# A graph network on one core: normed node values made before the adjacency, three strips, the preparations of the messages moved into the second convolution, and pools that wait by tile

## The chip, the cores and the metric

The program runs on one core of one Trainium2 chip. The metric is the device time of one execution in microseconds (us), as the median of several runs. Each profile is of one execution, with its own time beside its span. PE is TensorE (PEld its weight loads), DVE VectorE, ACT ScalarE, POOL GpSimd, SP SyncE; SPq, ACTq and POOLq are DMA issues of these engines.

## What is computed

There are N = 6250 nodes with 64 features and E = 206250 edges, sorted by their target `dst`. Every edge stands in both directions, and each node has one to itself. Ahead of each of four layers the node values are normed. Cut to what matters:

```python
h = maximum(layernorm(x), 0); x = x + conv(conv(h, W3, b3, relu), W4, b4)   # D^-1/2 (A+I) D^-1/2
h = maximum(layernorm(x), 0); x = x + segment_sum(norm * h[col], row)
h = maximum(layernorm(x), 0)
Vp = leaky_relu(leaky_relu(h) @ pAw + pAb) @ pBw + pBb
e = relu(relu(E @ w1 + b1) @ w2 + b2)
msg = sigmoid(e @ Bw + Bb) * Vp[src] + (e @ Cw + Cb)
x = x + sqrt(segment_mean(clip(msg, 1e-5) ** 2, dst))
h = maximum(layernorm(x), 0); acc = h
for _ in range(3): h = segment_sum(norm * h[row], col); acc = acc + h
x = x + acc / 4
```

## The kernel before

The nodes are padded to 49 blocks of 128, in 7 chunks of 7 blocks (`blocks(c)`, 896 nodes). The kernel builds the matrix A of edge counts, 6272 x 6272, as fp8, and every sum over edges but that of the messages is a product with it. Node values that are multiplied with A are split into three bf16 parts (`split`, L709: two copies on ACT, two subtractions on DVE for a chunk), kept in U3 or V3.

**Stage 1: edges to keys, degrees (L751 to L921).** The edge ends are combined to one number per edge, written to DRAM, and read back by 25 rough and 25 exact searches: `near` (a broadcast of samples), 25 comparisons on DVE (L802), then for each column group an indirect gather by POOL (L864), a comparison (L868), a second gather (L873), digits, transposes, and `key`. The loop at L871 also builds the first strip. When all 25 groups are done, the degrees follow (L904 to L919), and from them `norm0` and `norm3`.

**Stage 2: A in 14 strips of 448 columns, and the first convolution (L923 to L990).** First, for each chunk, `normed` (L691: three passes and two small steps on DVE, a square root on ACT, a last pass) of X, times `norm0`, and `split` into U3. `build(s, q)` makes 32 columns of strip s: two comparisons on DVE (L844, `hd` and `lo`), 16 matmuls into `p_a` (L853), two copies to fp8 on ACT (L857). 14 of these make a strip, and `convolve(s)` multiplies it with U3 (147 matmuls, L748), while strip s+1 is built. The strip goes to DRAM (L984). Every two strips `hidden(c)` turns the sums of one chunk into V3 by small matmuls and transposes (L737 to L967). `spool` has 2 strips.

**Stages 3 and 4: two gathers (`gather`, L998).** For each of 7 chunks, 7 pieces of A (128 x 7 x 896, loaded by SP, 8 buffers) are multiplied with V3 or U3: 343 matmuls (L1013) into four banks `p_acc`, opened by products with zeros (L1010) and summed up by DVE (L1021). Then `convolved` (L1035) finishes the chunk of the second convolution, norms it and splits it into a new U3; `turned` (L1053) in stage 4 adds the second layer, norms, and computes Vp by PE (L1062, L1067, L1073), ACT (L1065, L1069) and DVE (L1070, L1076, L1078), and SP writes it to DRAM (L1079).

**Preparations of the messages (L1085 to L1157).** Weights and biases are put into place (biases as three bf16 parts, L1113 to L1120). `src` and `dst` are loaded with `p` as the partition: each partition takes 8 edges of every one of 202 groups (L1125, L1127), runs of 32 bytes. From dst come a check that each group's targets lie in a window of 128 nodes (POOL's 194 memsets of `origin`, L1133, and L1136 to L1142 on DVE) and the `lane` of each edge (L1145, L1147).

**Stage 5: messages (L1158 to L1414).** 202 groups of 1024 edges go through a software pipeline, `slot(i)` (L1350): POOL fetches the rows of Vp by 8 indirect gathers (L1276, 4 buffers of `v`), PE, ACT and DVE take the edge features through the small network, gate them with v, square, and sum to the nodes. Beside this, PE and DVE compare A with its transpose, and PE does parts of the next layer's sums. On PE, ACT and DVE the order of this stage is written out by hand (`manual_schedule`, L1396). Everywhere else, and on POOL and SP throughout, a planner orders the instructions: it may run an instruction ahead of others on its engine when its inputs and its memory are free, and prefers those that come first in the program. Each engine then runs its list in order.

**Stage 6: the three propagations (L1417 to L1462)**, the first from sums already made, the others by `gather`.

Pools are opened and closed as a stack in SBUF and PSUM, so a new pool takes the memory of closed ones. By default, an instruction that first uses the new pool's memory waits for the pools that lay there before.

Of the kernel before, what the change touches and what calls it, by code (L numbers as in the profile page):

```python
# [8 lines left out]
F32 = mybir.dt.float32  # L9
BF16 = mybir.dt.bfloat16  # L10
# [6 lines left out]
P = 128  # L17
N = 6250
D = 64
# [597 lines left out]
def fast(ctx, tc, bad, x, src, dst, edge_attr, W3, b3, W4, b4, w1, b1, w2, b2, Bw, Bb, Cw, Cb,  # L617
# [48 lines left out]
    node = ctx.enter_context(tc.tile_pool(name="node", bufs=1))  # L666
    stat = ctx.enter_context(tc.tile_pool(name="stat", bufs=2))
# [3 lines left out]
    def blocks(c):  # L671
        return slice(c * CB, (c + 1) * CB)

    def over_features(v, n=CB):
        return v.unsqueeze(2).to_broadcast([P, n, D])
# [15 lines left out]
    def normed(h, X_c):  # L691

        m = stat.tile([P, CB], F32, name="m")
        nc.vector.tensor_reduce(m, X_c, axis=AX.X, op=OP.add)
        nc.vector.tensor_scalar_mul(m, m, 1.0 / D)
        nc.vector.tensor_sub(h, X_c, over_features(m))
        q = stat.tile([P, CB, D], F32, name="q")
        nc.vector.tensor_mul(q, h, h)
        v = stat.tile([P, CB], F32, name="v")
        nc.vector.tensor_reduce(v, q, axis=AX.X, op=OP.add)  # L700
        nc.scalar.activation(v, v, AF.Sqrt, bias=eps, scale=1.0 / D)
        nc.vector.reciprocal(v, v)
        nc.vector.scalar_tensor_tensor(h, h, 0.0, over_features(v), op0=OP.max, op1=OP.mult)
# [48 lines left out]
    nc.scalar.dma_start(X, x.rearrange("(b p) f -> p b f", p=P))  # L752
    early = ExitStack()
    early_pool = early.enter_context(tc.tile_pool(name="early_pool", bufs=1))
    with ExitStack() as ph:

        ipool = ph.enter_context(tc.tile_pool(name="ipool", bufs=1))
        with ExitStack() as first:
            dpool = first.enter_context(tc.tile_pool(name="dpool", bufs=1))
# [37 lines left out]
        npool = looked.enter_context(tc.tile_pool(name="npool", bufs=1))  # L797
# [11 lines left out]
        rpool = ph.enter_context(tc.tile_pool(name="rpool", bufs=3))  # L809
        opool = ph.enter_context(tc.tile_pool(name="opool", bufs=2))  # L810
        spool = ph.enter_context(tc.tile_pool(name="spool", bufs=2))
        wpool = ph.enter_context(tc.tile_pool(name="wpool", bufs=1))
# [13 lines left out]
        with ExitStack() as ps:  # L826
            psum = ps.enter_context(tc.tile_pool(name="ps0", bufs=1, space=PSUM))
            p = psum.tile([P, 512], F32, name="p_node")
            nc.tensor.transpose(p[:D, :P], W3_sb, ident)
            nc.vector.tensor_copy(W3T, p[:D, :P])  # L830
            p = psum.tile([P, 512], F32, name="p_node")
            nc.tensor.transpose(p[:, :D], W4_sb, ident[:D, :D])
            nc.vector.tensor_copy(W4T, p[:, :D])
# [90 lines left out]
            for c in range(NC):  # L924
                u = wpool.tile([P, CB, D], F32, name="z", bufs=2)
                normed(u, X[:, blocks(c), :])
                nc.vector.tensor_mul(u, u, over_features(norm0[:, blocks(c)]))
                split(u, U3, c)
# [97 lines left out]

    with ExitStack() as ph:
        wpool = ph.enter_context(tc.tile_pool(name="wpool", bufs=2))  # L1030
        U3 = of_nodes(node)
        with tc.tile_pool(name="apool", bufs=8) as apool, \
                tc.tile_pool(name="ps1", bufs=1, space=PSUM) as psum:

            def convolved(c, z):  # L1035
                add_whole(z, V3, c)
                nc.vector.tensor_mul(z, z, over_features(norm0[:, blocks(c)]))
                nc.vector.tensor_add(z, z, over_blocks(b4_r, CB))
                nc.vector.tensor_add(X[:, blocks(c), :], X[:, blocks(c), :], z)
                h = wpool.tile([P, CB, D], F32, name="h")  # L1040
                normed_and_split(h, U3, c, norm3)

            gather(apool, wpool, psum, V3, convolved)
# [6 lines left out]
        with tc.tile_pool(name="apool", bufs=8) as apool, \  # L1050
                tc.tile_pool(name="ps2", bufs=1, space=PSUM) as psum:
# [34 lines left out]
    late = ctx.enter_context(tc.tile_pool(name="late", bufs=1))  # L1086
    H = late.tile([P, NB, D], F32, name="H")
    U3 = of_nodes(node)
    part = ctx.enter_context(tc.tile_pool(name="part", bufs=1))
    Y = part.tile([P, CS, CW], F32, name="Y")  # L1090
    piece_pool = ctx.enter_context(tc.tile_pool(name="piece_pool", bufs=3))
    with ExitStack() as ph:
        cpool = ph.enter_context(tc.tile_pool(name="cpool", bufs=1))
        before = ExitStack()
        tpool = before.enter_context(tc.tile_pool(name="tpool", bufs=1))
        w1_d = diagonal(w1, "w1_d")
        w2_d = diagonal(w2, "w2_d")
        b1_c = column(b1, 2, "b1_c")
        b2_c = column(b2, 2, "b2_c")

        BC = cpool.tile([P, 4 * D], F32, name="BC")
        nc.vector.memset(BC, 0.0)
        for k in range(2):
            nc.scalar.dma_start(BC[k * D:(k + 1) * D, 2 * k * D:(2 * k + 1) * D], Bw)
            nc.scalar.dma_start(BC[k * D:(k + 1) * D, (2 * k + 1) * D:(2 * k + 2) * D], Cw)

        bias = tpool.tile([1, 4, 2, D], F32, name="bias")
        for k in range(4):
            nc.scalar.dma_start(bias[:, k, 0, :], Bb.unsqueeze(0))
            nc.scalar.dma_start(bias[:, k, 1, :], Cb.unsqueeze(0))  # L1110
        rest = tpool.tile([1, 4, 2, D], F32, name="rest")
        bias3 = [tpool.tile([1, 4, 2, D], BF16, name=f"bias{k}") for k in range(3)]
        nc.vector.tensor_copy(bias3[0], bias)  # L1113
        nc.vector.tensor_sub(rest, bias, bias3[0])
        nc.vector.tensor_copy(bias3[1], rest)
        nc.vector.tensor_sub(rest, rest, bias3[1])
        nc.vector.tensor_copy(bias3[2], rest)
        BC_b = cpool.tile([3, 8 * D], BF16, name="BC_b")
        for k in range(3):
            nc.sync.dma_start(BC_b[k:k + 1, :], bias3[k].rearrange("o a b f -> o (a b f)"))  # L1120
        ones = cpool.tile([3, P], BF16, name="ones")
        nc.vector.memset(ones, 1.0)

        src_g = cpool.tile([P, G, J], I32, name="src_g")
        nc.sync.dma_start(src_g, src.rearrange("(g p j) -> p g j", p=P, j=J))  # L1125
        dst_g = tpool.tile([P, G, J], I32, name="dst_g")
        nc.sync.dma_start(dst_g, dst.rearrange("(g p j) -> p g j", p=P, j=J))  # L1127

        origin = tpool.tile([P, G], F32, name="origin")
        g0 = 0  # L1130
        for g in range(1, G + 1):
            if g == G or window(g) != window(g0):
                nc.gpsimd.memset(origin[:, g0:g], float(window(g0) * QN))  # L1133
                g0 = g
        rel = tpool.tile([P, G, J], F32, name="rel")
        nc.vector.tensor_tensor(rel, dst_g, origin.unsqueeze(2).to_broadcast([P, G, J]),  # L1136
                                op=OP.subtract)
        off = tpool.tile([P, G, J], F32, name="off")
        nc.vector.tensor_scalar(off, rel, float(P), None, op0=OP.is_ge)
        nc.vector.tensor_scalar(rel, rel, 0.0, None, op0=OP.is_lt)  # L1140
        nc.vector.tensor_add(off, off, rel)
        nc.vector.tensor_reduce(missed[:, 1:2], off.rearrange("p g j -> p (g j)"), axis=AX.X,  # L1142
                                op=OP.add)

        nc.vector.tensor_scalar(dst_g, dst_g, P - 1, None, op0=OP.bitwise_and)  # L1145
        lane = cpool.tile([P, G, J], BF16, name="lane")
        nc.vector.tensor_copy(lane, dst_g)  # L1147
        own = cpool.tile([P, P // QN, 2], F32, name="own")
        nc.vector.memset(own[:, :, 0], 0.0)
        for q in range(P // QN):  # L1150
            nc.vector.memset(own[q * QN:(q + 1) * QN, :q + 1, 0], 1.0)
        nc.vector.tensor_scalar(own[:, :, 1], own[:, :, 0], -1.0, 1.0, op0=OP.mult, op1=OP.add)
        count = cpool.tile([P, P, J], BF16, name="count")
        nc.gpsimd.iota(count, pattern=[[1, P], [0, J]], base=0, channel_multiplier=0,
                       allow_small_or_imprecise_dtypes=True)

        before.close()  # L1157
        mpool = ph.enter_context(tc.tile_pool(name="mpool", bufs=3))  # L1158
        ps_a = ph.enter_context(tc.tile_pool(name="ps_a", bufs=1, space=PSUM))
# [255 lines left out]


    with ExitStack() as ph:  # L1417
        apool = ph.enter_context(tc.tile_pool(name="apool", bufs=6))
        wpool = ph.enter_context(tc.tile_pool(name="wpool", bufs=2))
        psum = ph.enter_context(tc.tile_pool(name="ps4", bufs=1, space=PSUM))  # L1420
        upool = ph.enter_context(tc.tile_pool(name="upool", bufs=1))
# [82 lines left out]
```

## Time and profile before

| What | us |
|---|---|
| median of 10 runs (lowest to highest) | 3639.87 (3636.82 to 3643.76) |
| profiled execution | 3635.89 |
| its span | 3633.8 |
| busy PE / DVE / ACT / POOL | 3042.0 / 1949.8 / 1243.6 / 1647.0 |
| first and last gather of messages begin | 1074.07, 3148.8 |
| searches begin to be read (L802) | 32.02 |
| first matmul of the first convolution | 151.21 |
| first matmul of `gather`, first time | 596.04 |

In a row of groups one reads line, engine, operation, output and inputs, count, then busy us and mean ns of one, then idle time of the engine just before them, with what ended it. In a timeline row one reads start, duration, engine, line and operation, and in brackets the idle time before it and its releaser. A row that spans a window gives the busy time of each engine in it and the clock that PE was granted as a share of the full one.

### The profile page before, as it was taken

What the parts mean: (1) busy time and instruction counts of PE and PEld (TensorE: products, weight loads), DVE (VectorE), ACT (ScalarE), POOL (GpSimd) and SP (SyncE); (2) the same over time, 40 slices, a digit from 0 to 9 for tenths busy, and PEclk for the clock granted to TensorE, in tenths of its full rate; (3) what the DMA queues carried; (4) which work ended last, traced back from release to release, by engine and by line L of the source; (5) the groups of instructions that cost most, each with busy time, mean ns of one, the idle gap of its engine ahead of it and who ended that gap; (6) DMA issues with size and microseconds to landing.
All of it is one profiled execution on the core that took longest, in us unless ns stands there. A gap on an engine that the chain in (4) does not pass through costs nothing.

```text
span 3633.8 us, 59188 instructions
## 1 busy us (share of the span) xinstructions
PE 3042.0 (84%) x24193; PEld 2135.9 (59%) x24193; DVE 1949.8 (54%) x3904; ACT 1243.6 (34%) x2031; POOL 1647.0 (45%) x1870
## 2 busy tenths in 40 slices
PE   1699999999957777778888788888887878799999
PEld 1466667999944444444444444454444444489999
DVE  5899993332235546555655655655655565531111
ACT  1477772000014334334444433444434344210000
POOL 4100000000027777777777777777777777500000
PEclk9699999999978888888888888888888988899999
DMA  3133335646572222323233223232332323256664
GB/s 112 53 95 94 95 95 174 196 173 197 177 93 73 73 67 67 88 70 94 70 90 85 78 70 88 76 88 70 96 80 78 94 69 79 80 161 196 196 205 143
DMA packets 280495, 388.75 MB, mean 107 GB/s; under 512 B 189225, under 2 KB 191331, under 8 KB 279955
## 3 DMA queue, kind: packets, MB, share of 16 engines
q1 hardware_dynamic: 222260, 323.17, 29.5%
q0 software_dynamic: 54112, 58.92, 8.0%
q8 instruction: 192, 3.15, 0.4%
q10 hardware_dynamic: 3840, 2.77, 0.3%
q14 instruction: 91, 0.75, 0.1%
HBM read 340.47 MB, written 44.24 MB: 106 GB/s over the span
## 4 chain that ended last, share of the span: by engine, by line
POOL 35%; PE 33%; issue 15%; DMA 9%; DVE 6%; ACT 1%; POOLq 0%; DVEq 0%; SPq 0%; ACTq 0%
POOL v L1276 34%; PE p_acc L1013 21%; DMA v<-Vp_dram,src_g 6%; PE p_sum L748 6%; PE p_a L853 3%; DVE hd L844 1%; DVE lo L844 1%; DMA dst_g<-in_dst 1%; PE p_node L739 1%; DMA near<-pairs,begin_i 1%; PE p_bc L1302 0%; PE p_node L957 0%; DMA run<-pairs,exact_i 0%; PE p_acc L1010 0%; PE p_node L962 0%
## 5 line engine op out<-in xcount | busy, mean ns | idle before, releaser
L1276 POOL DMA_INDIRECT v<-Vp_dram,src_g x1616 | 1583.5, 980 | 526.5 <-issue 458.0
L1013 PE MATMUL p_acc<-U,piece 128*128 128x192 bf16 x9604 | 815.7, 247 | 3.0 <-DMA piece<-A 3.0
L1013 PEld LDWEIGHTS <-piece 128*128 128x128 fp8e4 x9604 | 798.2, 98 | 14.7 <-DMA piece<-A 3.8
L1302 PE MATMUL p_bc<-BC,h 128*128 128x256 f32 x1616 | 584.3, 495 | 0.0
L1311 DVE TENSOR_TENSOR m<-gate,v 128x512 f32<-128x512 f32 x202 | 140.0, 693 | 760.2 <-DMA v<-Vp_dram,src_g 330.7
L1302 PEld LDWEIGHTS p_bc<-BC,h 128*128 128x128 f32 x1616 | 341.7, 234 | 156.2 <-issue 117.5
L1133 POOL MEMSET origin<- 128x1 f32 (+1 forms) x194 | 6.5, 97 | 906.9 <-PE p_acc L1013 906.9
L1318 ACT ACTIVATE m<-m 128x512 bf16<-128x512 f32 x202 | 127.2, 630 | 816.3 <-DVE m L1313 816.3
L1021 DVE TENSOR_REDUCE zg<-p_acc 128x128 f32<-128x384 f32 x112 | 56.8, 507 | 598.6 <-PE p_acc L1013 598.0
L748 PEld LDWEIGHTS <-U 128*64 128x64 bf16 x4116 | 233.5, 114 | 236.7 <-issue 93.2
L857 ACT ACTIVATE strip<-p_a 128x784 fp8e4<-128x784 f32 x392 | 301.8, 820 | 105.0 <-PE p_a L853 103.6
L1298 PE MATMUL p_bc<-BC_b,ones 3*128 3x512 bf16 x404 | 182.3, 451 | 169.3 <-DVE m L1312 169.1
L1298 PEld LDWEIGHTS <-ones 3*128 3x128 bf16 x404 | 37.5, 93 | 438.5 <-DVE m L1312 238.2
L1185 PEld LDWEIGHTS <-piece 128*128 128x128 fp8e4 x1372 | 116.0, 106 | 297.2 <-issue 279.5
L1185 PE MATMUL p_sum<-ident_b,piece 128*128 128x128 bf16 x1372 | 152.6, 235 | 163.7 <-DVE junk L1191 163.7
L1288 PE MATMUL p<-h,w_d 128*128 128x512 f32 x404 | 249.0, 701 | 39.4 <-ACT h L1292 39.4
L748 PE MATMUL p_sum<-piece,U 128*64 128x448 fp8e4 x2058 | 239.7, 377 | 39.2 <-DVE junk L1191 29.2
L1292 ACT ACTIVATE h<-p,b_c 128x512 f32<-128x512 f32 x404 | 255.7, 683 | 13.7 <-PE p L1288 13.7
L1191 DVE SCALAR_TENSOR_TENSOR junk<-p_sum,there 128x512 bf16<-128x512 f32 (+1 forms) x392 | 242.1, 618 | 21.4 <-DMA e<-in_edge_attr 8.0
L748 PE MATMUL p_sum<-strip,U 128*64 128x448 fp8e4 x2058 | 243.8, 365 | 8.9 <-ACT U L711 4.6
L844 DVE TENSOR_TENSOR lo<-count,key 128x2048 bf16<-128x2048 bf16 x196 | 238.2, 1215 | 0.0
L853 PEld LDWEIGHTS <-lo 128*128 128x128 bf16 x3136 | 164.9, 103 | 106.8 <-DVE lo L844 86.7
(189 smaller groups left out, 3471.4 us busy)
## 6 DMA issues: line engine op xcount, KB each, us to landing
piece<-A SPq DMA_DIRECT2D x249, 784.0 KB
e<-in_edge_attr SPq DMA_DIRECT2D x202, 256.0 KB
A<-strip SPq DMA_DIRECT2D x14, 2744.0 KB
v<-Vp_dram,src_g POOLq DMA_INDIRECT x1616
there<-A SPq DMA_DIRECT2D x28, 784.0 KB
pairs<-pair SPq DMA_DIRECT2D x1, 1616.0 KB
Vp_dram<-v SPq DMA_DIRECT2D x7, 224.0 KB
out<-X SPq DMA_DIRECT2D x6, 224.0 KB
```

What stands on the lines that cost most here:

```text
L748: nc.tensor.matmul(p[half * D:(half + 1) * D, :w], U3[:, b, k, :], at_block, start=(i < 2), stop=(i >= 3 * n - 2))
L844: nc.vector.tensor_tensor(t, of.unsqueeze(1).to_broadcast(t.shape), key[:, k, at:at + GB].rearrange("p (h j) -> p h j", j=GQ) .unsqueeze(2 ...
L853: nc.tensor.matmul(p[:, j, :2 * NB], lo[:, g // GQ, :, g % GQ], hd[:, g // GQ, :, g % GQ], start=True, stop=True)
L857: nc.scalar.activation(strips[s][:, :, col:col + 2 * SG].rearrange("p b (j l) -> p b j l", l=2), p[:, :, :2 * NB].rearrange("p j (b l) -> ...
L1013: nc.tensor.matmul(p[d // 2][:, d % 2 * 3 * D:(d % 2 + 1) * 3 * D], t[:, b, d * P:(d + 1) * P], U3[:, k * CB + b, :, :].rearrange("p t f - ...
L1185: nc.tensor.matmul(p[:, a - a0, :], held["here"][:, a, b * P:(b + 1) * P], ident_b, start=True, stop=True)
L1191: nc.vector.scalar_tensor_tensor(junk[:, :(a1 - a0) * P], p[:, :a1 - a0, :].rearrange("p a q -> p (a q)"), 15.5, there, op0=OP.min, op1=OP ...
L1276: nc.gpsimd.indirect_dma_start(out=v[:, j, :], out_offset=None, in_=Vp_dram[:, :], in_offset=bass.IndirectOffsetOnAxis(ap=src_g[:, g, j:j ...
L1288: nc.tensor.matmul(of[g][p], w, of[g].pop(x), start=True, stop=True)
L1292: nc.scalar.activation(of[g][t], of[g].pop(p), **how)
L1298: nc.tensor.matmul(p_bc[:, 4 * b:4 * b + 4].rearrange("p j o f -> p (j o f)"), ones, BC_b, start=True, stop=False)
L1302: nc.tensor.matmul(p_bc[:, 2 * q:2 * q + 2].rearrange("p j o f -> p (j o f)"), h2[:, q * P:(q + 1) * P], BC, start=False, stop=(k == 1))
```

## The change

Four things are changed, all in `fast`.

1. Every pool of `fast` other than `const` and `dram` is opened with `reuse_waits="tile"`: an instruction that first uses memory of closed pools waits for the tiles that lay in that memory, rather than for the closed pools as wholes. `spool` gets 3 buffers instead of 2 and lies at the right end of the memory. In the first PSUM pool the two small transposes at the start use `p_a` instead of `p_node`, so that `p_a` is the first to be placed there.
2. The normed values of all chunks are made into a tile `H0` before the searches' results are read; after the degrees only the product with `norm0` and the split are left.
3. The preparations become a function `prepared`, called by `convolved` of chunk 1 in stage 3. Their tiles lie at the right end (`cpool`, `tpool`); `cpool` stays until after the messages.
4. In it `src` and `dst` are loaded as long rows: 101 groups on 101 partitions, 4 KB each, in two halves, by ACT's queue. DVE casts each half to f32, turned to (g, j, p); PE transposes it, one of the 8 edges at a time (32 transposes in all); ACT copies the results back as integers, four at a time. The loads of `BC_b` move from SP's queue to ACT's.

```diff
-    spool = ph.enter_context(tc.tile_pool(name="spool", bufs=2))
+    spool = ph.enter_context(tc.tile_pool(name="spool", bufs=3, side="right", reuse_waits="tile"))
...
+            H0 = ipool.tile([P, NB, D], F32, name="H0")
+            for c in range(NC):
+                normed(H0[:, blocks(c), :], X[:, blocks(c), :])
...
                 u = wpool.tile([P, CB, D], F32, name="z", bufs=2)
-                normed(u, X[:, blocks(c), :])
-                nc.vector.tensor_mul(u, u, over_features(norm0[:, blocks(c)]))
+                nc.vector.tensor_mul(u, H0[:, blocks(c), :], over_features(norm0[:, blocks(c)]))
                 split(u, U3, c)
...
+    def prepared(psum):
+        cpool = apart.enter_context(tc.tile_pool(name="cpool", bufs=1, side="right", reuse_waits="tile"))
...
+        for k in range(3):
+            nc.scalar.dma_start(BC_b[k:k + 1, :], bias3[k].rearrange("o a b f -> o (a b f)"))
...
+        GH = G // 2
+        for ends, t in ((src, src_g), (dst, dst_g)):
+            for h in range(2):
+                rows_i = tpool.tile([GH, P, J], I32, name="rows_i", bufs=2)
+                nc.scalar.dma_start(rows_i, ends[h * GH * P * J:(h + 1) * GH * P * J].rearrange(
+                    "(g p j) -> g p j", p=P, j=J))
+                rows_f = tpool.tile([GH, J, P], F32, name="rows_f", bufs=2)
+                nc.vector.tensor_copy(rows_f, rows_i.rearrange("g p j -> g j p"))
+                for j0 in range(0, J, 4):
+                    p = psum.tile([P, 4, GH], F32, name="p_turn", bufs=2)
+                    for j in range(4):
+                        nc.tensor.transpose(p[:, j, :], rows_f[:, j0 + j, :], ident[:GH, :GH])
+                    nc.scalar.activation(
+                        t[:, h * GH:(h + 1) * GH, j0:j0 + 4],
+                        p.rearrange("p j g -> p g j"), AF.Copy)
...
             def convolved(c, z):
+                if c == 1:
+                    made.append(prepared(psum))
                 add_whole(z, V3, c)
...
-        nc.sync.dma_start(src_g, src.rearrange("(g p j) -> p g j", p=P, j=J))
...
-        nc.sync.dma_start(dst_g, dst.rearrange("(g p j) -> p g j", p=P, j=J))
...
+        cpool, w1_d, w2_d, b1_c, b2_c, BC, BC_b, ones, src_g, lane, own, count = made.pop()
```

All other lines of the preparations are moved as they are.

## The prediction

> **What bounds the kernel now.** The profiled execution took 3635.89 us, 3633.8 of them span; the median of the ten runs, 3639.87, is 4.0 above. I sum against 3635.89 and add the 4.0 at the end. I read the groups first, then stretches between the stages, then the timeline at the seams.
>
> ```profile
> L1276 POOL DMA_INDIRECT v<-Vp_dram,src_g x1616 | 1583.5, 980 | 526.5 <-issue 458.0
> L1013 PE MATMUL p_acc<-U,piece 128*128 128x192 bf16 x9604 | 815.7, 247 | 3.0 <-DMA piece<-A 3.0
> ```
>
> The 1616 gathers of the message stage start between 1074.07 and 3148.8, one every (3148.8 - 1074.07) / 1615 = 1.285 us; of POOL's idle time 458.0 us is "issue" and 34.4 the wait ahead of the first gather. So POOL paces over half of the span, and when its first gather starts, the end of that stage follows. PE paces the rest. By stretches (start:end, length, busy PE, weight load, DVE, ACT, POOL, granted clock, DMA share, GB/s):
>
> ```profile
> 150.00:180.00 30.00, 22.14 (x174) 10.92 (x174) 29.29 (x56) 12.72 (x24) 0.00 (x0) 0.75 0.00 1
> 180.00:300.00 120.00, 117.78 (x1415) 75.80 (x1416) 112.22 (x121) 86.02 (x120) 0.00 (x0) 0.97 0.35 95
> 565.00:596.00 31.00, 25.07 (x191) 16.78 (x187) 1.87 (x3) 5.07 (x9) 0.00 (x0) 0.82 0.84 291
> 800.00:840.00 40.00, 35.91 (x407) 34.74 (x407) 14.97 (x28) 1.75 (x4) 0.00 (x0) 0.96 0.82 305
> 1032.00:1075.00 43.00, 5.21 (x14) 3.00 (x14) 17.63 (x32) 1.58 (x3) 8.63 (x177) 0.54 1.30 85
> ```
>
> From 180 on PE is the bound of the first convolution (98% busy). It has holes at four seams: 150 to 180, where DVE is full; 565 to 596; 800 to 804; and 1032 to 1075, the largest. There the timeline shows
>
> ```profile
> 1030.65 0.94 DVE L1021 TENSOR_REDUCE zg<-p_acc 128x128 f32<-128x384 f32 x2 [0.60 <-PE p_acc L1013]
> ...
> 1049.71 0.30 ACT L701 ACTIVATE v<-v,eps 128x7 f32<-128x7 f32 x1 [42.32 <-DMA bias<-in_L_gnn_Bb]
> ...
> 1063.54 1.84 DVE L1136 TENSOR_TENSOR rel<-dst_g,origin 128x1616 f32<-128x1616 int32 x1 [4.74 <-DMA dst_g<-in_dst]
> ...
> 1066.01 0.39 SPq L1079 DMA_DIRECT2D Vp_dram<-v  x1
> ...
> 1071.40 1.83 DVE L1142 TENSOR_REDUCE missed<-off 128x1 f32<-128x1616 f32 x1
> ...
> 1074.07 0.97 POOL L1276 DMA_INDIRECT v<-Vp_dram,src_g  x1 [34.37 <-DMA piece<-A]
> ```
>
> The last chunk of the second gather still has to be turned into Vp, but its square root stands on ACT's queue behind the bias loads (13.5 us from the end of L700 at 1036.2), its last adds on DVE behind the wait for dst_g, and the gather starts 0.8 us after the last check of the preparations (1073.23), in whose memory its buffers lie. Put down to a piece, that last wait is DVE's.
>
> **Part 1, the preparations moved (e): -25 us.** For chunk 5 the same chain runs from the end of its sums (998.71) to the write of Vp (1010.08): 11.4 us. For the last chunk PE is cold: its three steps there took 1.08 + 2.07 + 2.05 instead of 0.66 + 1.12 + 1.16, 2.3 more. So the write is issued at 1031.6 + 13.6 = 1045.2, lands 2.3 later, and with the 0.8 above POOL starts near 1048.4 instead of 1074.07: 25.7 less, taken as 25 (20 if loads for the messages slip into the chain, 26 at best). What is late next is that chain itself. POOL's 194 memsets and the iota (8.6 us) leave this place too; they were done at 1039.7, so nothing.
>
> **The same work in the second convolution (c): +10 us.** DVE gets 1.84 + 1.83 + 1.83 + 4 x 0.99 (the lines on 1616 elements) + 2.6 for the biases + four casts of 1024 elements at about 1, together 16; between 596 and 800 it is busy 70 of 204, so the gathers cover it. ACT gets 8 evictions (0.55, like L732) beside 9 of 204 busy. PE has no cover: 32 transposes at 0.165 (L1062: four in 0.66) are 5.3, and each of 8 groups breaks into the sums. In the second gather three such groups of 2.94 us lengthen a chunk from 28.95 to 32.88, 0.33 a break, so 2.6: together 8 (0 if they fall into PE's holes, 16 at L731's 0.28 apiece with twice the breaks). The new loads have no row: [101 rows x 4 KB], four times. From below, like a piece (803 KB in 4.15 us at 800): 2.1 us; from above, all through one of 16 engines at what 565 to 596 gives (291 / 16 / 0.84 = 21.7 GB/s): 19.1. The third load is on ACT's queue and waits there for the cast of the first; behind it stand the square roots and splits of the convolution, behind these DVE's sums, and PE waits for both. Instructions whose memory is free have been run far ahead (L1406, last of the messages, ran at 1033), so the loads should start near 583 and the transposes come after chunk 1's sums, 70 us on; that covers four times 2.1, and nearly four times 19.1. I add 2 (0 to 76).
>
> The Trainium skill, "DMA: Bandwidth & Descriptors", section on why a DMA increments its semaphore by 16, speaks against the long rows: a transfer goes over the largest number of engines up to 16 that divides its outer dimension, which for 101 is one. At that page's 27 GiB/s I estimate 14.3 us a load, 57 for four; by it the transposes would wait if placed early, and (c) would grow to as much as 65. No row of this trace shows such a load.
>
> **Part 2, normed values first, three strips (a): -6 us.** From 130 to 180 DVE computes five of seven normed chunks at 3.4 us (seven lines of 0.61 to 0.62 and 0.16 to 0.20), 17 us; only two fitted earlier, into two buffers. PE waits meanwhile (30 - 22.14 = 7.9, and 2.2 more to 300). With H0 ready a chunk of U3 needs 1.85 of DVE, less than the 2.0 in which PE uses it up (21 matmuls at 0.096), so PE can fill these 10. The price: of the 17 us, 7.3 fit while DVE waits for "near" (24.7 to 32.0); the rest goes among the searches from 42 to 130, where DVE has 31 us idle in small pieces; I let 4 of it delay them. Bounds: -10 (nothing delayed) and +8 (all ten delayed, 2 regained). The third strip is worth nothing by itself: after 180 PE has no holes to fill.
>
> **Part 3, waits by tile (b, d): -8 and -3 us.** After the last strip's sums (579.86) PE has 10.2 us of small steps up to 594.75 and starts the first gather at
>
> ```profile
> 595.47 0.50 PE L1010 MATMUL p_acc<-zeros,ident_b 128*128 128x384 bf16 x1 [0.72 <-DVE z L966]
> ...
> 804.19 29.79 PE L1013 MATMUL p_acc<-U,piece 128*128 128x192 bf16 x343 [2.97 <-DMA piece<-A]
> ```
>
> p_acc then lies in the banks of p_a, free since 565, and six of seven pieces don't need the last chunk. PE's 6 idle us can be filled, and the small steps run warm (3.25 against 1.71 us for L962, and alike): up to 12, none if the pieces still come late; I take 8. At 800 the second gather's pieces are asked for only when the first is over: 3 us (0 to 4). Elsewhere 0 (-3 to +3).
>
> **Sum.** -6 - 8 + 10 - 3 - 25 = -32: 3603.9 for the profiled execution, 3608 as a median.
>
> **Rivals.**
> 1. *The searches pay for H0.* (a) is +8: 3622. For it: DVE is the engine they wait for. Against: 31 us idle.
> 2. *The long rows come late.* Transposes or ACT wait some 20 us: 3626. For it: 84% DMA share at 565 to 596, when these loads start. Against: the 70 us of sums ahead.
> 3. *The start is held by something else.* Only ACT's 13.5 is won at 1031, since the first gather or the write waits for other loads: 3619. For it: SP's queue is in order. Against: L1142 ends right before the gather.
> 4. *Slower: the long rows on the path.* All four loads at 19.1, one after another, with PE waiting for each: 76 instead of 2, so 3608 + 74 = 3682. From a wait of 34 us on the kernel is no faster. It needs the transposes ahead of the sums in PE's order, in the holes at 580 to 596, and each load through one engine.
>
> The change may also do its work and move nothing: if POOL's pace grew by 32 / 1616 = 0.02 us; nothing in it touches the gathers, so this has no chance of its own.
>
> **Numbers.** Forecast 0.56 (its own range 3590 to 3622), rival 1 0.13, rival 2 0.12, rival 3 0.08, rival 4 0.09, rest 0.02. A measurement tells 0.2% (7.3 us) from no change. Faster by more: 0.56 + 0.13 + 0.10 + 0.08 = 0.87; within: 0.02 of rival 2 and the rest, 0.04; slower: 0.09. The range reaches from all gains at their best with PE's transposes at half price (-10 - 12 + 4 - 4 - 26 - 3, so 3589) to the upper side of rival 2: 3589 to 3634, some 0.85 of the cases.
>
> **What would show it.** First gather near 1048, less what was won earlier (for part 1); PE idle under 2 us from 150 to 180, the L802 group still at 32 (part 2); first L1010 at 580 (part 3); transposes close together, no wait for rows_i or p_turn on PE or ACT in the first gather (c). Wrong makes it: a PE hole of tens of us between 580 and 700, L802 late, or a first gather after 1055.

## The result, and the profile after

The changed kernel takes 3659.15 us (median of 8 runs, 3654.9 to 3662.35) against 3638.88 for the kernel before on the same chips: a ratio of 1.0055 [1.0046, 1.0063]. The forecast was 3608. The profiled span grew from 3633.8 to 3656.5, by 22.7.

The same two groups, from the page of the changed kernel:

```profile
L1302 POOL DMA_INDIRECT v<-Vp_dram,src_g x1616 | 1583.5, 980 | 1009.7 <-issue 976.2
L1017 PE MATMUL p_acc<-U,piece 128*128 128x192 bf16 x9604 | 823.5, 248 | 24.9 <-DMA piece<-A 24.9
```

POOL's busy time is the same to the last digit. PE now waits 24.9 us for pieces, where it waited 3.0; 3.65 of them lie at the start of the second gather, where the 3.0 lay. The stretches of the changed kernel (columns as before: start:end, length, busy PE, weight load, DVE, ACT, POOL, clock, DMA share, GB/s):

```profile
150.00:180.00 30.00, 26.26 (x262) 16.02 (x263) 29.57 (x47) 19.19 (x31) 0.00 (x0) 1.00 0.01 2
180.00:300.00 120.00, 119.51 (x1495) 78.32 (x1496) 114.06 (x121) 89.87 (x124) 0.00 (x0) 1.00 0.35 95
587.00:680.00 93.00, 54.06 (x535) 51.49 (x534) 17.28 (x31) 2.90 (x6) 0.00 (x0) 0.74 0.36 130
1032.00:1075.00 43.00, 40.54 (x466) 38.78 (x464) 11.18 (x22) 1.58 (x3) 0.00 (x0) 1.00 0.25 77
```

The hole at 150 to 180 is half closed. A new one, far larger, lies at 587 to 680: PE works 54 of 93 us, at a clock of 0.74, and DMA moves only 130 GB/s. PE's timeline there, and DMA's parts of the chain that ended last, name the waits:

```profile
585.88 1.49 PE L1014 MATMUL p_acc<-zeros,ident_b 128*128 128x384 bf16 x4
...
605.07 1.10 PE L1077 MATMUL p_turn<-ident,rows_f 101*128 101x101 f32 x5 [17.70 <-DVE rows_f L1073]
...
633.47 14.74 PE L1017 MATMUL p_acc<-U,piece 128*128 128x192 bf16 x147 [8.62 <-DMA piece<-A]
656.08 2.42 PE L1017 MATMUL p_acc<-U,piece 128*128 128x192 bf16 x14 [7.71 <-DMA piece<-A]
675.19 18.41 PE L1017 MATMUL p_acc<-U,piece 128*128 128x192 bf16 x196 [4.91 <-DMA piece<-A]
```
```profile
586.79 37.79 DMA rows_i<-in_src
629.28 41.30 DMA rows_i<-in_dst
```

Five of the 32 transposes stand in PE's order ahead of the first sums. They wait 17.70 us for the first cast, and that for its load. After them PE waits three times for pieces, 21.2 together: 38.9 in all. The first line of the chain runs from the issue of the second load to its landing, the other from that of the fourth. The four loads run one behind the other, from 582.79 to 670.58: 22 us for each 413.7 KB (101 x 4096 bytes), where a piece of 803 KB took 4.15. In a stretch with only such a load in flight, the row of the windows is

```profile
590.00:602.00 12.00, 0.00 (x0) 0.00 (x0) 0.87 (x2) 0.00 (x0) 0.00 (x0) 0.50 0.06 26
```

The mean share of the 16 DMA engines is 0.06, which is one engine of 16, and it moves 26 GB/s. The other fifteen rest, although SP has asked for only two pieces by then, and there are eight buffers. Here is the first row of pieces on SP's queue in the kernel before, and then rows of the changed kernel, each from a window of its own:

```profile
579.89 4.07 SPq L1007 DMA_DIRECT2D piece<-A  x8
```
```profile
603.98 0.80 SPq L1011 DMA_DIRECT2D piece<-A  x2
...
624.79 1.43 SPq L1011 DMA_DIRECT2D piece<-A  x3
...
647.79 1.27 SPq L1011 DMA_DIRECT2D piece<-A  x3
...
670.64 4.09 SPq L1011 DMA_DIRECT2D piece<-A  x8
```

Before the change the first eight pieces were asked for within 4 us. Now one is asked for at 579.23, one at 586.16, and the next only whenever a long load has landed (603.92, 624.59, 647.78, 670.58). The list of what SP's queue waited for, in total, times and longest, has

```profile
SPq L1011 <- DMA rows_i<-in_dst: 43.1, 2, 21.6
...
SPq L1011 <- DMA BC_b<-bias: 20.0, 1, 20.0
SPq L1011 <- DMA rows_i<-in_src: 17.4, 1, 17.4
```

The numbers of the semaphores (the counters by which instructions wait for each other) in the trace say how a load of ACT's queue can hold up SP's. The DMAs of both queues take the same eight semaphores in turns, and one is asked for only when the last with its semaphore has landed. The piece of 603.98 has the semaphore of the first load, those of 647.79 and 670.64 have those of the third and fourth; that of 624.79 has the semaphore of a small load of biases, whose last part landed right behind the second load (624.78). That a piece also shares the engine of the load counts for less: the 16 engines each mark the landing of their part of a piece, and for the pieces of 624.79 and 647.79, on which PE waited, the last mark came 4.0 and 3.6 us after the other fifteen; for pieces behind the last long load it was at most 1.2.

The bill, from the starts of the same instructions in both profiles:

| Stretch | before | after | difference |
|---|---|---|---|
| start to the last strip's sums (a) | 565.70 | 557.19 | -8.5 |
| from there to chunk 2 of the first gather (b, c) | 93.5 | 143.9 | +50.4 |
| chunk 2 to the start of the second gather (d) | 141.2 | 140.6 | -0.6 |
| second gather, start of messages (e) | 273.7 | 249.4 | -24.3 |
| first to last gather of messages | 2074.75 | 2074.6 | -0.1 |
| last gather to the end of the span | 485.0 | 490.9 | +5.9 |

From the end of the last sums to the first gather of messages alone, (e) went from 42.5 to 17.1; that gather is now

```profile
1091.03 0.97 POOL L1302 DMA_INDIRECT v<-Vp_dram,src_g  x1 [517.61 <-issue]
```

The last row of the table is a loss that no term of the prediction had. Timeline of the changed kernel's end, of SP and of DVE:

```profile
3158.61 16.69 SPq L1481 DMA_DIRECT2D piece<-A  x6
```
```profile
3173.78 0.69 DVE L1337 TENSOR_TENSOR m<-gate,v 128x512 f32<-128x512 f32 x1 [9.98 <-DMA v<-Vp_dram,src_g]
```

The last stage's pieces are asked for 7.0 us before POOL issues its last gather (3165.64), and the rows of that gather are used 8.1 us after. In the kernel before the pieces came long after it (3165.70 against 3148.82), and its last rows were used 3.1 us after it:

```profile
3165.70 2.96 SPq L1453 DMA_DIRECT2D piece<-A  x6
```

### The profile page after: what moved, and what is told of

Read it like the earlier page. It is cut to its first block, busy times and chain, and to the rows that moved or that the text cites. A ratio compares the mean times of both kernels' runs of the same rounds, so it can differ in the third digit from the quotient of the medians.

```text
span 3656.5 us, 59236 instructions
## 1 busy us (share of the span) xinstructions
PE 3051.8 (83%) x24225; PEld 2140.9 (59%) x24225; DVE 1952.5 (53%) x3908; ACT 1248.6 (34%) x2039; POOL 1647.1 (45%) x1870
## 4 chain that ended last, share of the span: by engine, by line
POOL 33%; PE 33%; issue 14%; DMA 10%; DVE 7%; ACT 2%; ACTq 0%; POOLq 0%; DVEq 0%; SPq 0%
POOL v L1302 33%; PE p_acc L1017 20%; DMA v<-Vp_dram,src_g 7%; PE p_sum L748 6%; PE p_a L858 3%; DVE hd L849 1%; DMA rows_i<-in_dst 1%; DMA rows_i<-in_src 1%; DVE lo L849 1%; PE p_node L739 1%; PE p_bc L1328 1%; DMA near<-pairs,begin_i 1%; PE p_node L961 0%; DMA run<-pairs,exact_i 0%; PE p_node L966 0%
## 5 line engine op out<-in xcount | busy, mean ns | idle before, releaser
L1302 POOL DMA_INDIRECT v<-Vp_dram,src_g x1616 | 1583.5, 980 | 1009.7 <-issue 976.2
L1017 PE MATMUL p_acc<-U,piece 128*128 128x192 bf16 x9604 | 823.5, 248 | 24.9 <-DMA piece<-A 24.9
L1217 DVE SCALAR_TENSOR_TENSOR junk<-p_sum,there 128x512 bf16<-128x512 f32 (+1 forms) x392 | 242.1, 618 | 22.8 <-PE p_sum L1211 14.2
L858 PE MATMUL p_a<-hd,lo 128*128 128x98 bf16 x3136 | 195.7, 217 | 33.1 <-DVE lo L849 31.2
```

Source lines behind the costliest of these rows:

```text
L858: nc.tensor.matmul(p[:, j, :2 * NB], lo[:, g // GQ, :, g % GQ], hd[:, g // GQ, :, g % GQ], start=True, stop=True)
L1017: nc.tensor.matmul(p[d // 2][:, d % 2 * 3 * D:(d % 2 + 1) * 3 * D], t[:, b, d * P:(d + 1) * P], U3[:, k * CB + b, :, :].rearrange("p t f - ...
L1217: nc.vector.scalar_tensor_tensor(junk[:, :(a1 - a0) * P], p[:, :a1 - a0, :].rearrange("p a q -> p (a q)"), 15.5, there, op0=OP.min, op1=OP ...
L1302: nc.gpsimd.indirect_dma_start(out=v[:, j, :], out_offset=None, in_=Vp_dram[:, :], in_offset=bass.IndirectOffsetOnAxis(ap=src_g[:, g, j:j ...
```

## The experiments

My theory was then: a load with 101 as its outer size goes through one DMA engine and takes some 19 us; PE waits for it directly (the five transposes) and through the pieces, which need that engine too. The last clause falls short of SP's rows above: the pieces were asked for late.

**1. Each long load as two.**

```diff
-  nc.scalar.dma_start(rows_i, long_rows)
+  for lo_, hi_ in ((0, 96), (96, GH)):
+      nc.scalar.dma_start(rows_i[lo_:hi_], long_rows[lo_:hi_])
```

> Each load of 101 rows is issued as two, of 96 and of 5 rows; the order of work on PE is the same. Theory A (a load of 101 rows runs through one DMA engine, some 19 us each; PE waits for it 17.7 us at its first transposes and 21 us more for pieces of A that come late beside it): the loads land in 2 to 5 us, the four PE waits between 587 and 680 (38.9 us) shrink to under 6, and the time is 3608 to 3620. Theory B (the price is the place: transposes ahead of the first sums, and the preparations' loads on ACT's queue, however fast the rows come): 3645 to 3660.

Measured: 3616.84 us, ratio 0.9933 [0.9917, 0.995]. PE waits 4.5 us for the first turn, and for pieces only at the start of the second gather (3.5). So one line turns a loss of 20 us into a gain of 22, with the same bytes and the same transposes in the same place of PE's order. Theory B is out. Whether it is the row count or the smaller size of each load that counts, run 4 tells. The same stretch of PE's timeline:

```profile
591.07 1.10 PE L1079 MATMUL p_turn<-ident,rows_f 101*128 101x101 f32 x5 [4.54 <-DVE rows_f L1075]
```

**2. The moved preparations with the old short runs** (32 bytes each, straight into `src_g` and `dst_g`; no long rows, casts or transposes).

> The preparations stay in the second convolution, but src and dst are loaded as before in runs of 32 bytes, without casts and transposes. Theory A: no load through one engine, so the large hole goes; the two loads take some 27 us each over all engines, beside the pieces: 3605 to 3630. Theory B for the transposes: the same, 3605 to 3630; theory B for ACT's queue: 3640 to 3660, since the biases still stand there behind loads that are slower to issue (10.5 us for one before).

Measured: 3629.32, ratio 0.9968 [0.9955, 0.998]. That is at the upper end of theory A, and theory B for ACT's queue is out. Short runs at this place are better than the 101-row loads and 12 us worse than split long rows. The check on DVE stands ahead of a chunk's reductions and waits for `dst_g`, and PE waits 14.02 us for these. DVE's timeline:

```profile
630.14 1.84 DVE L1076 TENSOR_TENSOR rel<-dst_g,origin 128x1616 f32<-128x1616 int32 x1 [26.84 <-DMA dst_g<-in_dst]
```

**3. Long loads that nothing reads.** Split loads, and besides them the four loads of 101 rows, into a tile that nothing reads.

```diff
+  unread = tpool.tile([GH, P, J], I32, name="unread", bufs=2)
+  nc.scalar.dma_start(unread, long_rows)
```

> As the kernel with two loads, and beside it four loads of 101 rows into tiles that nothing reads: only their use of the DMA engines is left. Theory A says that this alone makes pieces late: 15 to 25 us above the kernel with two loads. Theory C (the rows are slow, but only PE's own wait for the transposes costs, 17.7 us, and the late pieces are its echo): within 5 us of the kernel with two loads.

Measured: 3649.11, ratio 1.0031 [1.002, 1.0042]: 32 us more than the split loads, above what I expected. No instruction reads these loads, yet PE waits 25.6 us for pieces in the first gather (29.1 with the 3.5 at the start of the second, which the split loads have too). The longest:

```profile
636.91 11.07 PE L1017 MATMUL p_acc<-U,piece 128*128 128x192 bf16 x98 [3.62 <-DMA piece<-A]
657.89 10.83 PE L1017 MATMUL p_acc<-U,piece 128*128 128x192 bf16 x98 [9.91 <-DMA piece<-A]
678.78 6.59 PE L1017 MATMUL p_acc<-U,piece 128*128 128x192 bf16 x49 [10.06 <-DMA piece<-A]
```

98 matmuls are two pieces: two arrive in each 21 us, where PE would use up five. The run does not leave the engine alone, though, since the unread loads take semaphores as well. SP's queue waits for them,

```profile
SPq L1011 <- DMA unread<-in_src: 42.4, 2, 22.4
SPq L1011 <- DMA unread<-in_dst: 40.2, 2, 20.1
```

and asks for two pieces each at 628.55, 649.46 and 670.44, right after an unread load has landed (628.48, 649.40, 670.38). So it shows that long loads make the pieces late when no transpose waits for them, and theory C is out; it does not show that the shared engine does it.

**4. 106 and 96 rows instead of twice 101**, each in one load.

```diff
-  for h in range(2):
+  for g_, GH in ((0, 106), (106, G - 106)):
```

> The changed kernel with one load per part, but parts of 106 and 96 rows instead of twice 101 (the transposes' sizes follow). Theory A, that the number of engines follows from the divisors of the row count: the loads of 96 rows land as fast as a piece, the two of 106 go through two engines and take about half of the 19 to 20 us of the 101-row loads, so some 9 to 10 us; TensorE waits for the first turn 5 to 12 us (5.0 with split loads, 17.7 with 101 rows), for the pieces under 10 us together (3.5 and 21.2), and the time is 3617 to 3630. Theory B, that a load of some 100 rows of 4 KB is slow whatever the count is, and splitting helps because of the smaller pieces: the 96-row loads take 18 us or more too, and the time is 3645 to 3660.

Measured: 3622.59, ratio 0.9955 [0.9938, 0.9971]; PE waits 10.6 us for the first turn and not once for a piece between 586 and 806. The first load of 106 rows, with more bytes than one of 101, is there 14.0 us after its issue (582.47 to 596.45; 21.1 with 101 rows), longer than the 9 to 10 I expected. The engine count is what theory A says, though. While hardly anything else is in flight, the share is 0.12, two engines of 16, at twice the rate of one:

```profile
593.00:596.30 3.30, 0.00 (x0) 0.00 (x0) 0.00 (x0) 0.00 (x0) 0.00 (x0) 0.50 0.12 50
```

At 50 GB/s the 434.2 KB would take 8.7 us, an estimate; in 587 to 591, with a piece and the load of 96 rows beside it, the share was 0.82 to 1.00. So theory A holds in what decides: more bytes over two engines are there sooner than fewer over one, and the waits for the first turn follow (101 rows, 106, split into 96 and 5: 17.7, 10.6, 4.5). The first load of 96 rows was slower here than theory A had it (10.9 us; 5.0 with split loads): fourteen of its parts landed after 6.2 us, the last two right behind the load of 106. DVE's timeline:

```profile
596.48 1.08 DVE L1073 CAST rows_f<-rows_i 106x1024 f32<-106x1024 int32 x1 [5.93 <-DMA rows_i<-in_src]
```

**5. The cover that the prediction counted on.** The 101-row loads as they are, but the casts wait for the sums of chunk 1, so that no transpose lies ahead.

```diff
   rows_f = tpool.tile([GH, J, P], F32, name="rows_f", bufs=2)
+  nc.vector.tensor_copy(rows_f[:1, 0, :1], z[:1, 0, :1])
```

> The changed kernel with its four loads of 101 rows as they are, but the conversions of the long rows to f32 made to wait for the sums of chunk 1 of the first gather, so that no transpose lies ahead of the first sums in TensorE's order: the loads start near 583 and the transposes come some 70 us later, which is just what the prediction took as its cover. The prediction's step: with that cover the loads cost 2 us; the time is 3615 to 3622 and TensorE waits under 5 us between 585 and 760. My theory now: the transposes at the front are only the smaller half of the harm; each load keeps one engine busy for some 19 us and every piece needs that engine too, so the pieces come late all the same, and what TensorE no longer waits for the first turn (17.7 us) it partly waits for pieces; waits for pieces of 20 to 35 us, time 3637 to 3655.

Measured: 3671.29, ratio 1.0093 [1.0076, 1.011], slower than both expectations. The waits for pieces are 21.3, as in the changed kernel, so the late transposes gained nothing there. But the third and fourth load need the buffers that the casts free, so they now start at 670.69, and the transposes behind them stand in PE's order, as its timeline shows:

```profile
692.74 1.58 PE L1078 MATMUL p_turn<-ident,rows_f 101*128 101x101 f32 x8 [12.86 <-DVE rows_f L1073]
708.71 1.58 PE L1078 MATMUL p_turn<-ident,rows_f 101*128 101x101 f32 x8 [13.75 <-DVE rows_f L1074]
```

My edit added a wait of its own, so its time doesn't test the prediction's step; run 7 does.

**6. The loads themselves late**, when the buffers of pieces are full: the small copy goes into `rows_i`, so that each load waits for it.

> The changed kernel with its four loads of 101 rows, each made to wait for the sums of chunk 1 of the first gather, so that they begin near 650, when the eight buffers of pieces are full. During the 76 to 80 us of four such loads TensorE uses up some 19 pieces; at two pieces to each 20 us, as seen beside the unread loads, 8 arrive, and 8 lie ready. My theory: the eight buffers cover about half; TensorE waits 8 to 25 us for pieces, mostly in the last of the four loads, and the time is 3622 to 3642. The rival, that full buffers hide the loads: waits under 4 us, time 3613 to 3620. The other rival, that the place doesn't matter: waits of 29 us or more as beside the unread loads, time 3645 or more.

Measured: 3682.41, ratio 1.0116 [1.0099, 1.0133]. The time is the second rival's, but the mechanism is none of the three. PE waits 0.0 for pieces in the first gather and 57.6 for transposes, since each group of eight is placed right behind the point at which its load seems due, and PE does nothing else meanwhile. Its timeline:

```profile
668.16 1.61 PE L1078 MATMUL p_turn<-ident,rows_f 101*128 101x101 f32 x8 [18.94 <-DVE rows_f L1074]
684.23 1.58 PE L1078 MATMUL p_turn<-ident,rows_f 101*128 101x101 f32 x8 [11.90 <-DVE rows_f L1074]
700.34 1.58 PE L1078 MATMUL p_turn<-ident,rows_f 101*128 101x101 f32 x8 [12.16 <-DVE rows_f L1074]
718.94 1.58 PE L1078 MATMUL p_turn<-ident,rows_f 101*128 101x101 f32 x8 [14.62 <-DVE rows_f L1074]
```

It says nothing on whether full buffers cover the pieces. It shows the loads almost alone, though. Their casts start at 667.03, 683.00, 699.11 and 717.71, so the second and the third load, each behind the one before, took 16.0 and 16.1 us: 413.7 KB / 16.0 us = 25.9 GB/s, where the pieces reached 418 GB/s in 590 to 610 of the same profile. That is one engine of 16 (418 / 16 = 26), and so says the share in the row of the third load:

```profile
684.00:698.00 14.00, 3.96 (x24) 3.56 (x24) 2.10 (x5) 1.01 (x2) 0.00 (x0) 0.62 0.06 26
```

**7. Run 5 with four buffers for the long rows**, so that no load waits for a cast (`bufs=4` for `rows_i`).

> The kernel with late conversions (transposes behind the sums of chunk 1) and four buffers instead of two for the long rows, so that all four loads of 101 rows are asked for near 582 and none waits for a conversion; nothing stands in TensorE's order for them until some 70 us later. Theory P, that each such load makes the pieces late by itself while it runs: 21 us of waits for pieces came with two loads at this place, 29 with four unread ones; with four here TensorE waits 29 to 45 us for pieces, under 8 us for turns, and the time is 3640 to 3660. Theory O, that only what waits for the loads in an engine's order costs, and pieces are late beside them only as long as their buffers are empty, in the first 20 us: waits for pieces of 15 to 25 us, under 8 us for turns, time 3628 to 3638. The prediction's step, that 70 us of cover hide the four loads: time 3613 to 3620.

Measured: ratio 1.0029 [0.9991, 1.0066]. When this run was made, the kernel before took 4163.27 us and this one 4174.16, most of it more between the gathers of the messages (POOL idle for 1487.9 us there, 1009.7 in the changed kernel above), so the ratio and the waits are read and not the times. PE waits 0.4 us for turns, and for pieces 41.7 in the first gather (45.1 with the start of the second), near theory P's upper end. From PE's timeline, the two longest:

```profile
635.72 17.80 PE L1017 MATMUL p_acc<-U,piece 128*128 128x192 bf16 x196 [29.88 <-DMA piece<-A]
660.41 6.94 PE L1017 MATMUL p_acc<-U,piece 128*128 128x192 bf16 x49 [6.89 <-DMA piece<-A]
```

SP asks for a piece at 593.08 and for the next at 626.89, when the second load has landed (626.83). With the cover just as the prediction described it, the four loads still cost 42 us of PE instead of 2. Theory P has the number; as in run 3, the late asking lies behind it.

**8 and 9. What of (a) is whose.** Split loads, and either two strips (`bufs=2` for `spool`), or the normed values made after the degrees (no H0).

> The changed kernel with split loads and two strips instead of three. My theory, as in the prediction: the third strip is worth nothing by itself, because TensorE has no holes to fill after 180 us; then the last strip's sums begin within 1.5 us of the 557 to 558 us of the changed kernel, and the time stays within 3 us of the 3616.8 of the split loads alone. The rival: a good part of the 8.5 us that the end of the first convolution came earlier is the third strip's, since with it building a strip no longer waits for the products of the one two before; then the last strip's sums begin 3 to 8 us later and the time is 3620 to 3625.

> The changed kernel with split loads, three strips, and the normed values made after the degrees as in the kernel before. My theory: the normed values first are what moved the end of the first convolution by 8.5 us, net of the 5.7 us that they delay the searches; without them the searches begin near 32 us again, TensorE waits some 8 us between 150 and 180 us again, the last strip's sums begin near 565 us, and the time is 3622 to 3628. The rival: most of the gain comes from the third strip, and the delay of the searches eats up what H0 gives; then the last strip's sums begin at 553 to 559 us and the time is 3612 to 3618.

Measured: 3617.6, ratio 0.9938 [0.9921, 0.9955], with two strips, and 3627.79, ratio 0.9964 [0.9951, 0.9976], without H0. The last strip's sums begin at 556.11 with split loads alone and at 555.88 with two strips: the third strip is worth nothing. Without H0 they begin where they did before the change (565.70), as PE's timeline has it:

```profile
565.93 14.16 PE L748 MATMUL p_sum<-strip,U 128*64 128x448 fp8e4 x147 [0.38 <-ACT strip L859]
```

So (a) comes from H0; its parts are below.

**10. Split loads, and all pools waiting as wholes again.**

> As the kernel with two loads, with all pools waiting for closed pools as wholes, as before the change. If waits by tile are worth what the prediction said (11 us): 11 us above the kernel with two loads. From the profile of the changed kernel (first gather begins 14.5 us after the last strip's sums instead of 15.6; pieces of the second gather come as late as before; last gathers of messages 5 to 6 us later beside early pieces): 2 to 8 us below it.

Measured: 3610.48, ratio 0.9917 [0.99, 0.9933], 6.4 below the split loads alone. With tile waits the first message gather starts 2.5 us earlier (1048.28 against 1050.76), but from there to the last one it takes 2.8 longer, and from the last one to the end 493.1 instead of 488.1. Tile waits lose more at the end than they gain at the seams.

**11. Seven buffers of pieces, tile waits kept, but the last stage's four pools waiting as wholes.**

> The changed kernel with split loads, with 7 instead of 8 buffers of pieces in both gathers, and with the four pools of the last stage waiting for closed pools as wholes again. My theory on the seam between the gathers: with 8 buffers the last of 49 pieces lies in buffer 0, which the first piece of the next gather takes, and the queue is in order, so tile waits gain nothing; with 7 buffers the last piece lies in buffer 6, the first pieces of the second gather are asked for from about 785 us on while the first still sums, and TensorE's wait of 3.5 us at 800 goes. On the tail: with tile waits the last stage's pieces are asked for beside the last gathers of the message stage and hold back their rows; as wholes, the stretch from the start of the last gather to the end of the span is 485 to 488 us again instead of 493. Together 3607 to 3610. The rival on the seam: one buffer less makes the pieces late inside the gathers, or the wait at 800 stays since it is the next U3 that is awaited; then the second gather starts no earlier, and the time is 3611 to 3616.

Measured: 3606.36, ratio 0.9911 [0.9894, 0.9927]. Both parts hold, and the time is just below the range that I gave. PE goes from one gather into the next without a wait, and the first message gather starts 4.4 us earlier than with split loads alone; the end takes 486.7 instead of 493.1, with the rows of the last gather used 3.1 us after it again. PE's timeline:

```profile
800.18 0.93 PE L1014 MATMUL p_acc<-zeros,ident_b 128*128 128x384 bf16 x4
800.96 28.46 PE L1017 MATMUL p_acc<-U,piece 128*128 128x192 bf16 x343
```

**12. Run 11 with the casts of run 5.**

> The kernel with split loads, seven buffers and a last stage that waits for whole pools, with the transposes also kept behind the sums of chunk 1. If the 4.9 us that TensorE still waits for the first turn there are on the path, they go, and the time is 3600 to 3604; if the first pieces come no earlier than the turns, TensorE waits for them instead and the time stays at 3605 to 3608.

Measured: 3602.63, ratio 0.9899 [0.9883, 0.9916], the fastest kernel here: with split loads the late casts do what run 5 meant. The wait ahead of the first turns is gone, and the second gather starts 4.9 us earlier than in run 11 (795.33). In its page the group of sums has no wait left:

```profile
L1017 PE MATMUL p_acc<-U,piece 128*128 128x192 bf16 x9604 | 815.0, 246 | 0.0
```

## Why the prediction was wrong

The failed step is in **(c): the stall of the new loads, taken as 2 us** "(0 to 76)" because "the loads should start near 583 and the transposes come after chunk 1's sums, 70 us on; that covers four times 2.1, and nearly four times 19.1". Each load did cost the upper end and more (21 to 23 us; 19.1 in the bound). Two things were missed:

- *The order.* Of 32 transposes 27 did come after chunk 1's sums (693 to 698), but five were put ahead of the first sums, where PE had a hole: 17.7 us. The prediction named that place, "in the holes at 580 to 596", as the condition of rival 4, and gave it 0.09.
- *The pieces, put at nothing without a reason.* The cover was thought of as time for the load; but the covering sums need pieces, and SP's queue asked for these only as the long loads landed, since its DMAs and ACT's share semaphores (80.5 us of SP's waits, for the loads and a small one behind them). PE waited 21.2 us for pieces so, 25.6 beside loads that nobody reads, 41.7 with all transposes late.

With the 38.9 us of waits PE also turned cold: in 587 to 680, at a granted clock of 0.74, a matmul took 54.06 / 535 = 0.101 us, and 98.38 / 1144 = 0.086 with split loads in 590 to 690, at 0.97; so I estimate 535 x 0.015 = 8 more. The transposes are a lesser item: 4.5 us busy where I counted 8 with their breaks. The stretch with split loads:

```profile
590.00:690.00 100.00, 98.38 (x1144) 96.83 (x1145) 42.18 (x67) 7.16 (x15) 0.00 (x0) 0.97 0.67 228
```

The weighing was at fault too. Between 2.1 us "like a piece" and 19.1 "through one engine", the row count itself was in the diff. The Trainium skill, "DMA: Bandwidth & Descriptors", section "Why a DMA increments its semaphore by 16 and not by 1", says that the number of engines is the largest one up to 16 that divides the outer sizes of both sides. The runs agree: a share of 0.06, one of 16, for 101 rows (the changed kernel, run 6) and of 0.12 for 106 (run 4). The estimate from the page's rate, 14.3 us a load, is short of the 16.0 measured nearly alone and the 21 to 23 beside pieces. I had cited it, and left its time out of the forecast since my cover seemed to make it harmless.

The other terms:

- **(a) -6: right in size,** -8.5 (bounds -10 to +8), and it comes from H0 as said: without H0 it is gone (run 9), and the third strip is worth nothing (run 8). Its parts were off, and cancel partly by luck. The searches came 5.7 us later (37.68 after 32.02), where I had said "still at 32" in one place and allowed 4 in another, and the first convolution began 6.4 later. From its first matmul to the last strip's sums the two kernels have (columns as before)

```profile
151.20:565.70 414.50, 403.72 (x4897) 258.19 (x4898) 397.36 (x443) 298.28 (x417) 0.00 (x0) 0.97 0.30 83
```
```profile
157.57:557.19 399.62, 396.15 (x4898) 256.16 (x4899) 384.38 (x412) 296.65 (x412) 6.51 (x194) 1.00 0.32 86
```

PE is idle for 3.5 us instead of 10.8, so 7.3 of the counted 10 were won, and the same matmuls take 7.6 less, at a granted clock of 1.00 instead of 0.97, a gain that no term had: 6.4 - 7.3 - 7.6 = -8.5. At 150 to 180 PE's idle time is 3.7, not under 2.
- **(b) -8: wrong by size,** about -1: from the end of the last strip's sums to the first L1014 it is 14.5 us after 15.6. "PE's 6 idle us can be filled" (5.5 by the rows) failed: the small steps still stand ahead of the gather in PE's order, and as cold as before (L966 takes the same 3.25 as L962 did).
- **(d) -3: 0.** The second gather's pieces were still asked for when the first was over (841.87, PE's wait 3.65). Run 11 shows the reason that I had overlooked: 49 pieces in 8 buffers end in buffer 0, which the next gather's first piece takes, and SP's queue is in order. With 7 buffers the wait is gone.
- **(e) -25: right,** -25.4. The chain from the last sums to the write of Vp took 13.8 us; 13.6 was worked out from chunk 5 and the cold steps.
- **Elsewhere 0 (-3 to +3): wrong,** +5.9 at the end. Waits by tile let the last stage's pieces start beside the last gathers (runs 10 and 11). The prediction looked at what a wait taken away lets start at two seams and not at the third.

One bound in (c) was added up wrongly, without bearing on the result: 32 transposes at 0.28 and 16 breaks at 0.33 make 14.2, not 16.

**The rivals.** Rival 4 came in part. Each load did go through one engine, and transposes did stand ahead of the sums, but five of 32, so PE waited directly for one load (17.7) and not for four. The other 21.2 came through the pieces, a way that no rival had. With the 8 for the clock that is 47 of its 76, and it decided as it said, "from a wait of 34 us on the kernel is no faster". Rival 2 had the size of the direct wait, "some 20 us", but not its reason, a busy DMA: the share in 590 to 602 is 0.06. Rivals 1 and 3 did not come: (a) and (e) are whole. With the terms as measured, -8.5 - 1.1 + 51.5 - 0.6 - 25.4 + 5.9 gives +21.8 of the 22.7; 51.5 is the stretch of (b) and (c) less (b), and the 38.9, 8 and 4.5 above make 51.4 of it. The rest lies in small stretches of the second gather.

What stays open: whether full buffers of pieces could cover a one-engine load, since in run 6 PE stood at the transposes instead; and what such a load would cost if the pieces had semaphores of their own, which no run tried.

## What to carry to other kernels

Before a transfer is priced, look at its outer size: with 101 rows it took 16 us nearly alone and 21 to 23 beside pieces, and as 96 and 5 rows with the same bytes it left a wait of 4.5, or none when the casts came late (run 12). Cover for a slow transfer must be checked twice, once for who waits for it in an engine's order, and once for which transfers of the covering work are asked for only when it has landed. The list of what the issuing queue waited for shows that, when the engine's own list only says "DMA piece". And where a wait is taken away, follow each queue to what now starts earlier: it may find its buffer still taken (49 pieces in 8 buffers), or run into a transfer that is on the path (the last gathers of the messages).

## What was not expected of the hardware

- A load of 101 rows keeps one DMA engine of 16 busy: 16.0 us for 413.7 KB nearly alone, at 26 GB/s with a mean share of 0.06, and 21 to 23 us beside the pieces.
- What shares that engine is late only by its last part: 3.6 and 4.0 us for the two pieces above that PE waited for beside a long load.
